# Another order of the seven Strassen products in a fused GAT and attention kernel

## The chip, the cores and the metric

The kernel runs on one core of one Trainium2 chip. The metric is device time in microseconds of one execution, the median of several runs. TensorE (PE) does matrix products, its weight loads are shown apart (PEld), VectorE (DVE), ScalarE (ACT) and GpSimd (POOL) do the elementwise work, and SyncE (SP) issues most of the transfers; ACT issues some as well.

## The reference

64 graphs of 256 nodes with 256 features pass through two layers, all in fp32.

```python
# layer 0, graph attention, adj is 0 or 1
h = gat(gat(x, adj, W1, a1), adj, W2, a2)          # softmax over nodes of leaky_relu scores, masked by adj
h = layernorm(x + h, g_ln1, b_ln1)
x = layernorm(h + relu(h @ w_ff1 + b_ff1) @ w_ff2 + b_ff2, g_ln2, b_ln2)     # 256 -> 1024 -> 256
# layer 1, attention of 8 heads with a value matrix per relation r
q, k = x @ Wq + bq, x @ Wk + bk
attn = softmax(q @ k.T / sqrt(32))
out = sum_r (attn * (adj == r)) @ (x @ Wv[r] + bv[r])
x = layernorm(x + out @ Wo + bo, g1, beta1)
out = layernorm(x + gelu(x @ W1 + b1) @ W2 + b2, g2, beta2)
```

With entries of 0 and 1 only two of the four relations occur, and the kernel has a path for that, `narrow_path`, which is the one that runs; a check of the data decides at its end whether the general path must follow.

## The kernel before, in words

A unit is two graphs, that is 512 rows in four blocks of 128. There are 32 units. `turn(y_, x_, z)` (L1226) works on three neighbouring units at once: the attention and the second feed-forward layer of unit y, the first feed-forward layer of unit x = y + 1, and the graph attention of unit z = y + 2. So each turn has three independent streams, whose pieces are interleaved by hand. The last two turns lack z, or z and x. A prologue (L1498 to L1532) brings the first units in.

The order is written out. `manual_schedule` (L1271) keeps the program's order on PE, SP, DVE and ACT within a turn that has a unit x; POOL is ordered by the planner, and around the border between two turns DVE and ACT of both may interleave. [...]A transfer issued by ACT stands in ACT's queue as well.

Three kinds of matrix product are done by Strassen's scheme, seven products of half-size quarters instead of eight: the projections q/k and v (`Projections`, L1006), the first half of each feed-forward layer (`hidden_seven`, L869) and its second half (`HiddenOut`, L957, not changed). Four sums of quarters are taken on the moving side beforehand (L880 to L886 and L1017), the sums of weights once at the start.

In `hidden_seven` the products come in halves a and b. Each half has two PSUM banks. Bank `two` receives product 2, then, overwritten, 5, and 3 is accumulated onto 5. Bank `one` receives 1, then 6, 7 and 4 accumulated onto it. The four output quarters (o, b) arise from what is read out between the products: quarter (0,0) is 2 (copied by ACT, L907) plus 1 (added by DVE, L910); quarter (1,1) is 5 (copied) plus bank one after 7 (added); quarter (0,1) is bank two after 3 (copied) plus bank one after 6 (added); quarter (1,0) is bank one after 4. A product may enter a bank only when the reader of what stood there is done. Then comes the function, ReLU in the first layer and Gelu in the second: "r" applies it to (0,0) and (0,1) of a half in two activations of 512 columns (L941), "s" to quarter (1,1) in two of 256 columns (L916), and product 4 is read through the function directly. The names "2a", "7b" in the order strings are product and half; each is two matrix multiplies (four PE records in the trace). For q and v, "q5" or "v6" name the same products of `Projections.step` (L1042); copies and adds have lines L1036 and L1040.

The places where the order is written: L1278 to L1309 for the projections together with quad 0 of the scores (`scores`, `powers` for the exponentials on ACT, L1093; `masks` for the multiplies by adjacency, L1097, and `totals`, L1102, on DVE), the calls of `first(...)` from L1322 to L1351 for unit x's first layer, and `second(...)` from L1438 to L1458 for unit y's second layer. Around these stand layer norms: `moments` and `norm` (L820, L830) with statistics on DVE and a power on POOL, `offsets` (L843) on DVE, `applied_norm` (L847) on ACT or, for two blocks of unit x, on POOL.

The transposed features hT that a layer multiplies are made by `normed_features` (L689): DVE transposes blocks of 32 by 32 (L694), then twelve transfers and four POOL copies put the pieces in place. For the first layer all twelve transfers are issued by SP, for the second layer (L1407) six by SP and six by ACT, after ACT has done `scaled` (L789) for unit z.

Of the kernel before, what the change touches and what calls it, by code (L numbers as in the profile page):

```python
# [16 lines left out]
P = 128  # L17
# [368 lines left out]
def narrow_path(  # L386
# [443 lines left out]
    def norm(u, l, y, blocks=range(T), mv=None):  # L830
# [3 lines left out]
        mv = moments(u, l, y, blocks if mv is None else blocks[len(blocks) // 2:], mv)  # L834
# [34 lines left out]
    def hidden_seven(u, l, hT, w, bi, func, d, tt):  # L869
# [39 lines left out]
        def added(h, o, b):  # L909
            mark["added"] = nc.vector.tensor_tensor(out(h, o, b), pair(one[h]), out(h, o, b), ALU.add)  # L910
# [8 lines left out]
        def step(name):  # L919
# [5 lines left out]
            elif n == "1":  # L925
                one[h] = bank(f"h1a{u}_{l}_{h}")
                product(one[h], h, a11, quarter[0][0], True)
                added(h, 0, 0)
# [4 lines left out]
            elif n == "3":  # L933
                product(two[h], h, s4, quarter[1][1], False)
                copied(h, 0, 1, two[h])
            elif n == "6":
                product(one[h], h, s2, moving(1), False)
                added(h, 0, 1)
# [3 lines left out]
            elif n == "7":  # L942
                product(one[h], h, s3, moving(2), False)
                added(h, 1, 1)
            elif n == "s":
                done(h, 1, 1)
            else:
                product(one[h], h, a22, moving(3), False)
                done(h, 1, 0, one[h])
# [56 lines left out]
    class Projections:  # L1006
# [31 lines left out]
        def added(s, x, o, b):  # L1038
            y = s.out(x, o, b)
            mark["projected"] = nc.vector.tensor_tensor(y, s.one[x].rearrange("p (i n) -> p i n", i=2), y, ALU.add)  # L1040

        def step(s, x, n):  # L1042
# [12 lines left out]
            if n == 2:  # L1055
                s.copied(x, 0, 0, ps)
                s.added(x, 0, 0)
            elif n == 5:
                s.copied(x, 1, 1, ps)
            elif n == 3:  # L1060
                s.copied(x, 0, 1, ps)
            elif n == 6:
                s.added(x, 0, 1)
            elif n == 7:
                s.added(x, 1, 1)
            elif n == 4:
                s.copied(x, 1, 0, ps)
# [158 lines left out]
    def turn(y_, x_, z):  # L1226
# [46 lines left out]
        with order:  # L1273
# [4 lines left out]
            p("q1 v1 q2")  # L1278
            if X:
                applied_norm(X["y"], *n, [0])  # L1280
            p("v2")
            if X:
                applied_norm(X["y"], *n, [1])
            p("q5")
            if X:
                applied_norm(X["y"], *n, [2])
                applied_norm(X["y"], *n, [3])
                X["hT"] = normed_features(x_, 0, X["y"])
            scores(0, (0,))
            p("v5")  # L1290
            powers(0, (1,))
            if z + 1 < NG:
                load_x(z + 1)
            p("q3 v3")
            powers(0, (2, 3))
            if waiting:
                w, wy = waiting[0]
                last = moments(w, 3, wy, range(NB))
            if X:
                masks(0, (0,))  # L1300
            p("q6 v6 q7 v7")
            if X:
                masks(0, (2,))
# [5 lines left out]
            p("q4 v4")  # L1309
            if waiting:  # L1310
                last = norm(w, 3, wy, mv=last)
            steps = first_hidden(x_) if X else None
            if waiting:
                offsets(*last)
            scores(1)
            masks(1)
# [12 lines left out]
            sums(1)  # L1329
            if X:  # L1330
                shares(0)
            first("3a 6a", 1)
# [4 lines left out]
            first("2b 1b")  # L1337
            masks(2, (2,))
            first("5b 7a 3b ra 6b")
            totals(2)  # L1340
            first("4a 7b rb")
# [4 lines left out]
            first("sa sb", 2)  # L1346
# [50 lines left out]
            if Z:  # L1397
# [3 lines left out]
                Z["m"].scaled(WH)  # L1401
            if X:
# [31 lines left out]
            if X:  # L1434
                out.add(4)
                n = norm(x_, 1, X["y"], mv=n)
            h1 = Y["h1"] = work.tile([P, FB, TN], F32, tag="h1", name=f"h1{y_}_1", bufs=1)
            second("2a 1a 2b 1b")  # L1438
            second("5a 5b")
            if X:  # L1440
                offsets(*n)
                applied_norm(X["y"], *n, [0])
            if Z:
                affine(y, rg3, rb3)
            second("3a")
            if X:
                applied_norm(X["y"], *n, [1])
            second("3b")
            if X:
                applied_norm(X["y"], *n, [2, 3], True)  # L1450
            second("6a 6b ra rb 7a 7b")
            if X and not Z:
                affine(y, rg3, rb3)
            if Z:
                X["hT"] = normed_features(x_, 1, X["y"], natural=True)
            elif X:
                X["hT"] = with_ones(to_features(X["y"], f"h2T{x_}", (nc.vector.tensor_copy,) * 2))
            second("sa sb 4a 4b")  # L1458
# [130 lines left out]
```

## Time and profile before

| | us |
|---|---|
| median of 3 runs | 3044.08 (3042.89 to 3045.79) |
| the profiled execution's own time | 3043.91 |
| its span, first to last instruction | 3042.3 |
| PE busy | 3000.0 |
| DVE busy | 2645.7 |
| ACT busy | 1684.9 |
| POOL busy | 679.8 |
| one copy of a bank, ACT, 128x512 (L907) | 0.585 |
| one add of a bank, DVE, 128x512 (L910) | 0.685 |
| one mask multiply, DVE, 128x1024 pairs (L1097) | 1.237 |
| one exponential, ACT, 128x512 (L1093) | 0.600 |

Busy means that the engine executed something; PE's weight loads overlap its multiplies and are shown apart. The ends of multiplies are modelled, so a busy PE may hold short waits. The chain is followed back from the last instruction to what released each step; it says which work set the end. A view of waits gives, for each engine and line, what ended the time before it. The mean granted clock of TensorE was 0.995.

### The profile page before, as it was taken

To read this page: it belongs to the slowest core of one execution; us is meant where nothing else is said; L and a number is where in the kernel's file an instruction comes from. 1 tells how busy PE (TensorE), PEld (TensorE's weight loads), DVE (VectorE), ACT (ScalarE), POOL (GpSimd) and SP (SyncE) were. 2 spreads that over 40 slices of the span, in tenths; PEclk is the share of its full clock that TensorE was granted. 3 is DMA by queue.
4 is the path that set the end of the run, shared out by engine and by line. 5 is a ranking of instruction groups with operands and counts; after the bars stand their busy time and mean duration, and the time that the engine had idled before them with its cause. 6 is when DMAs were issued, how large, how long until landed. Compare 5 with 4: busy or idle time off the path is not lost.

```text
span 3042.3 us, 58414 instructions
## 1 busy us (share of the span) xinstructions
PE 3000.0 (99%) x22192; PEld 2459.6 (81%) x22192; DVE 2645.7 (87%) x5025; ACT 1684.9 (55%) x3404; POOL 679.8 (22%) x930
## 2 busy tenths in 40 slices
PE   7999999999999999999999999999999999999998
PEld 6788888888787888787888878887878887878876
DVE  5788988888898889898889888898988898988887
ACT  4455555655655555555555455556555555555553
POOL 4222221222211222212222112222112222122211
PEclk8999999999999999999999999999999999999999
DMA  5011111211111211111111112111112111121000
GB/s 147 13 35 36 37 39 25 44 37 39 34 35 32 44 37 39 33 27 43 40 37 36 40 25 44 38 39 33 34 35 44 36 38 35 25 45 37 19 13 16
DMA packets 428402, 113.24 MB, mean 37 GB/s; under 512 B 364586, under 2 KB 427604, under 8 KB 428116
## 3 DMA queue, kind: packets, MB, share of 16 engines
q1 hardware_dynamic: 418076, 102.20, 15.3%
q10 hardware_dynamic: 8984, 6.19, 0.8%
q8 instruction: 178, 2.92, 0.4%
q0 software_dynamic: 1056, 1.05, 0.1%
q14 instruction: 108, 0.88, 0.1%
HBM read 56.78 MB, written 16.78 MB: 24 GB/s over the span
## 4 chain that ended last, share of the span: by engine, by line
PE 90%; DVE 7%; ACT 1%; DMA 1%; POOL 1%; issue 0%; SPq 0%; DVEq 0%; POOLq 0%; ACTq 0%
PE yf L987 22%; PE h1a L898 15%; PE h1b L898 12%; PE po L1112 8%; PE qk L1053 7%; PE v L1053 7%; PE sp L1084 4%; PE xpp L740 4%; PE yop L811 4%; PE ygp L811 3%; PE zo L1115 2%; PE hpp L800 2%; DVE s L775 2%; DVE yt L694 1%; DVE eaq L973 1%; DVE y L995 1%
## 5 line engine op out<-in xcount | busy, mean ns | idle before, releaser
L907 ACT COPY h<-h1b 128x512 f32<-128x512 f32 x384 | 224.5, 585 | 349.4 <-PE h1b L898 342.6
L910 DVE TENSOR_TENSOR h<-h1a,h 128x512 f32<-128x512 f32 x384 | 262.9, 685 | 114.6 <-PE h1a L898 108.8
L1097 DVE TENSOR_TENSOR ea<-e,aT 128x1024 f32<-128x1024 f32 x256 | 311.2, 1237 | 2.9 <-ACT e L1093 2.6
L855 ACT ACTIVATE y<-y,nm,rs 128x256 f32<-128x256 f32 x450 | 249.8, 597 | 114.4 <-DVE nm L845 110.1
L1093 ACT ACTIVATE e<-sp 128x512 f32<-128x512 f32 x512 | 270.8, 600 | 28.1 <-PE sp L1084 21.4
L1036 ACT COPY qk<-qk 128x512 f32<-128x512 f32 x128 | 75.1, 587 | 339.0 <-PE qk L1053 339.0
L711 POOL COPY hT<-yt 32x256 f32<-32x256 f32 x244 | 203.2, 833 | 184.9 <-DVE yt L694 172.6
L837 POOL TENSOR_SCALAR rs<-mv 128x4 f32<-128x4 f32 (+1 forms) x134 | 33.3, 248 | 841.0 <-DVE mv L827 625.3
L826 DVE BATCH_NORM_STATS2 st<-y 128x6 f32<-128x256 f32 x512 | 207.3, 407 | 4.5
L995 DVE TENSOR_TENSOR y<-yf,y 128x256 f32<-128x256 f32 x448 | 183.2, 409 | 29.5 <-PE yf L987 29.4
L1125 POOL TENSOR_TENSOR low<-low,rq 128x16 f32<-128x16 f32 x64 | 13.9, 218 | 810.4 <-DVE rq L1124 810.4
L867 DVE TENSOR_TENSOR y<-y,rb 128x1024 f32<-128x1024 f32 (+1 forms) x130 | 167.0, 1284 | 3.2
L941 ACT ACTIVATE h<-h,cols 128x512 f32<-128x512 f32 x256 | 167.0, 714 | 1.5 <-DVE h L910 1.1
L864 DVE TENSOR_TENSOR y<-y,rg 128x1024 f32<-128x1024 f32 (+1 forms) x130 | 161.6, 1243 | 1.2 <-ACT y L855 1.1
L1102 DVE TENSOR_TENSOR es<-e 128x1024 f32<-128x1024 f32 x128 | 155.8, 1217 | 0.0
L703 POOL COPY hT<-yt 32x256 f32<-32x256 f32 x120 | 114.9, 958 | 169.3 <-DVE yt L694 165.1
L838 POOL TENSOR_TENSOR rs<-rs,mhalf 128x4 f32<-128x4 f32 (+1 forms) x134 | 146.9, 1096 | 8.3
L1084 PE MATMUL sp<-qk 32*128 32x256 f32 x2048 | 146.6, 400 | 0.4 <-DVE qk L1040 0.3
L742 ACT COPY xp<-xpp 128x260 f32<-128x260 f32 x128 | 45.4, 385 | 172.6 <-PE xpp L740 172.5
L694 DVE STREAM_TRANSPOSE yt<-y 128x256 f32<-128x256 f32 x364 | 136.0, 418 | 4.5
L1112 PE MATMUL po<-e,v 128*32 128x256 f32 x2048 | 136.3, 384 | 0.0
L898 PE MATMUL h1a<-tt,wf 128*128 128x256 f32 x512 | 134.2, 386 | 0.3 <-DVE h L910 0.3
(280 smaller groups left out, 7589.6 us busy)
## 6 DMA issues: line engine op xcount, KB each, us to landing
hT<-yt SPq DMA_DIRECT2D x912, 32.0 KB, 1.9
y<-in_x_dram SPq DMA_DIRECT2D x32, 512.0 KB, 4.5
xq<-in_x_dram SPq DMA_DIRECT2D x240, 64.0 KB, 2.1
aq<-in_adj_dram SPq DMA_DIRECT2D x240, 64.0 KB, 2.3
out_dram<-y SPq DMA_DIRECT2D x30, 512.0 KB, 2.9
hT<-yt ACTq DMA_DIRECT2D x180, 32.0 KB, 1.9
wf<-in_L_gnn_w_ff_dram SPq DMA_DIRECT2D x2, 1024.0 KB, 7.6
w<-in_L_gnn_W_dram SPq DMA_DIRECT2D x2, 1024.0 KB, 7.9
```

The source lines that it names most:

```text
L811: nc.tensor.matmul(ps[:, i * F:(i + 1) * F], lhs(t, k), rhs(b, k), start=(k == 0), stop=(k == n - 1))
L855: mark["normed"] = nc.scalar.activation(y[:, t, :], y[:, t, :], AF.Identity, bias=nm[:, t:t + 1], scale=rs[:, t:t + 1])
L898: nc.tensor.matmul(ps[:, i * N:(i + 1) * N], w_[:, f * P:(f + 1) * P], m, start=first and i == 0, stop=True, skip_group_check=True)
L907: mark["copied"] = nc.scalar.copy(out(h, o, b), pair(ps))
L910: mark["added"] = nc.vector.tensor_tensor(out(h, o, b), pair(one[h]), out(h, o, b), ALU.add)
L987: nc.tensor.matmul(s.ps[n][:, i * F2:(i + 1) * F2], a[:, k, i * P:(i + 1) * P], w_[:, k, :], start=n in (1, 2, 5) and i == 0 and k == 0, s ...
L995: mark["out"] = nc.vector.tensor_tensor(yq, s.ps[n][:, :F].rearrange("p (i f) -> p i f", i=NB), yq, ALU.add)
L1053: nc.tensor.matmul(ps[:, i * N:(i + 1) * N], l, r, start=n in (1, 2, 5) and i == 0, stop=True, skip_group_check=True)
L1084: nc.tensor.matmul(ps[a][:, j * N:(j + 1) * N], k_[hp, m, j0:j0 + P], q[hp, m, b * N:(b + 1) * N], start=True, stop=True)
L1093: nc.scalar.activation(e[:, a, :], ps[a], AF.Exp, scale=isd)
L1097: nc.vector.tensor_tensor(ea[:, a:a + 2, :], e[:, a:a + 2, :], ab[:, None, :].to_broadcast([P, 2, NB * N]), ALU.mult)
L1112: nc.tensor.matmul(po[hp, m * N:(m + 1) * N], vs[:, hp], w[:, a, j * N:(j + 1) * N], start=(n == 0), stop=(n == len(terms) - 1))
```

## The change

The sixth product's bank is copied into quarter (0,1) and the third product's bank is added to it, where before the third was copied and the sixth added. So 6 can come before 3, and the order strings change: in both feed-forward layers and in the projections. In the second layer Gelu is applied per quarter: "c" to (0,0), "d" to (0,1) and "s" to (1,1), two activations of 256 columns each, and an activation of one column with Gelu is issued right after `scaled`. The norms, masks, moments and the transposes of features around these products move as well; `norm` gets an argument that says which blocks still lack statistics.

```diff
--- before.py
+++ after.py
@@ -827,11 +827,11 @@
             nc.vector.bn_aggr(mv[:, t, :], st[:, t, :])
         return mv
 
-    def norm(u, l, y, blocks=range(T), mv=None):
+    def norm(u, l, y, blocks=range(T), mv=None, rest=range(NB, T)):
 
         n, t0 = f"{u}_{l}_{blocks[0]}", blocks[0]
         bt = slice(t0, t0 + len(blocks))
-        mv = moments(u, l, y, blocks if mv is None else blocks[len(blocks) // 2:], mv)
+        mv = moments(u, l, y, blocks if mv is None else rest, mv)
         rs = work.tile([P, T], F32, tag="rs", name=f"rs{n}")
         nm = work.tile([P, T], F32, tag="nm", name=f"nm{n}")
         nc.gpsimd.tensor_scalar(rs[:, bt], mv[:, bt, 1], EPS, 0.0, op0=ALU.add, op1=ALU.add)
@@ -906,8 +906,8 @@
 
             mark["copied"] = nc.scalar.copy(out(h, o, b), pair(ps))
 
-        def added(h, o, b):
-            mark["added"] = nc.vector.tensor_tensor(out(h, o, b), pair(one[h]), out(h, o, b), ALU.add)
+        def added(h, o, b, ps):
+            mark["added"] = nc.vector.tensor_tensor(out(h, o, b), pair(ps), out(h, o, b), ALU.add)
 
         def done(h, o, b, ps=None):
             for i in range(2):
@@ -925,25 +925,25 @@
             elif n == "1":
                 one[h] = bank(f"h1a{u}_{l}_{h}")
                 product(one[h], h, a11, quarter[0][0], True)
-                added(h, 0, 0)
+                added(h, 0, 0, one[h])
             elif n == "5":
                 product(two[h], h, s1, moving(0), True)
                 copied(h, 1, 1, two[h])
                 mark["fifth"] = mark["copied"]
             elif n == "3":
                 product(two[h], h, s4, quarter[1][1], False)
-                copied(h, 0, 1, two[h])
+                added(h, 0, 1, two[h])
             elif n == "6":
                 product(one[h], h, s2, moving(1), False)
-                added(h, 0, 1)
+                copied(h, 0, 1, one[h])
             elif n == "r":
                 for f in range(2 * h, 2 * h + 2):
                     nc.scalar.activation(d["h1"][:, f, :], d["h1"][:, f, :], func, bias=bi[:, f:f + 1])
             elif n == "7":
                 product(one[h], h, s3, moving(2), False)
-                added(h, 1, 1)
-            elif n == "s":
-                done(h, 1, 1)
+                added(h, 1, 1, one[h])
+            elif n in "cds":
+                done(h, *{"c": (0, 0), "d": (0, 1), "s": (1, 1)}[n])
             else:
                 product(one[h], h, a22, moving(3), False)
                 done(h, 1, 0, one[h])
@@ -1035,9 +1035,9 @@
         def copied(s, x, o, b, ps):
             nc.scalar.copy(s.out(x, o, b), ps.rearrange("p (i n) -> p i n", i=2))
 
-        def added(s, x, o, b):
+        def added(s, x, o, b, ps):
             y = s.out(x, o, b)
-            mark["projected"] = nc.vector.tensor_tensor(y, s.one[x].rearrange("p (i n) -> p i n", i=2), y, ALU.add)
+            mark["projected"] = nc.vector.tensor_tensor(y, ps.rearrange("p (i n) -> p i n", i=2), y, ALU.add)
 
         def step(s, x, n):
             a11, a12, a22, s1, s2, s3, s4 = wqks if x == "q" else wvs
@@ -1052,19 +1052,8 @@
                 l, r = (w[:, i * P:(i + 1) * P], m) if x == "q" else (m[:, i * P:(i + 1) * P], w)
                 nc.tensor.matmul(ps[:, i * N:(i + 1) * N], l, r, start=n in (1, 2, 5) and i == 0, stop=True,
                                  skip_group_check=True)
-            if n == 2:
-                s.copied(x, 0, 0, ps)
-                s.added(x, 0, 0)
-            elif n == 5:
-                s.copied(x, 1, 1, ps)
-            elif n == 3:
-                s.copied(x, 0, 1, ps)
-            elif n == 6:
-                s.added(x, 0, 1)
-            elif n == 7:
-                s.added(x, 1, 1)
-            elif n == 4:
-                s.copied(x, 1, 0, ps)
+            to = {1: (0, 0), 2: (0, 0), 5: (1, 1), 6: (0, 1), 3: (0, 1), 7: (1, 1), 4: (1, 0)}[n]
+            (s.added if n in (1, 3, 7) else s.copied)(x, *to, ps)
 
         def __call__(s, names):
             for n in names.split():
@@ -1275,45 +1264,40 @@
             if X:
                 n = X.pop("n")
                 offsets(*n)
-            p("q1 v1 q2")
+            p("q2 v2 q1 v1")
             if X:
-                applied_norm(X["y"], *n, [0])
-            p("v2")
-            if X:
-                applied_norm(X["y"], *n, [1])
+                applied_norm(X["y"], *n, [0, 1, 2, 3])
+                X["hT"] = normed_features(x_, 0, X["y"])
             p("q5")
-            if X:
-                applied_norm(X["y"], *n, [2])
-                applied_norm(X["y"], *n, [3])
-                X["hT"] = normed_features(x_, 0, X["y"])
-            scores(0, (0,))
-            p("v5")
-            powers(0, (1,))
+            scores(0, (0, 1))
             if z + 1 < NG:
                 load_x(z + 1)
-            p("q3 v3")
-            powers(0, (2, 3))
             if waiting:
                 w, wy = waiting[0]
                 last = moments(w, 3, wy, range(NB))
+            p("v5 q6")
+            powers(0, (2,))
+            p("v6")
+            powers(0, (3,))
             if X:
-                masks(0, (0,))
-            p("q6 v6 q7 v7")
+                masks(0)
+            p("q3 q7")
+            p("v7")
             if X:
-                masks(0, (2,))
                 totals(0)
             else:
                 with behind("projected"):
                     masks(0)
                     totals(0)
-            p("q4 v4")
+            p("v3 q4 v4")
+            steps = first_hidden(x_) if X else None
             if waiting:
                 last = norm(w, 3, wy, mv=last)
-            steps = first_hidden(x_) if X else None
+            scores(1)
+            masks(1, (0,))
             if waiting:
                 offsets(*last)
-            scores(1)
-            masks(1)
+            masks(1, (2,))
             totals(1)
             if Z:
                 early(z)
@@ -1327,23 +1311,24 @@
                 first("2a 1a 5a", 1)
             scores(2)
             sums(1)
+            first("6a")
             if X:
                 shares(0)
-            first("3a 6a", 1)
+            first("3a", 1)
             if not X:
                 with behind("out"):
                     shares(0)
             masks(2, (0,))
-            first("2b 1b")
+            first("2b ra 1b 7a")
             masks(2, (2,))
-            first("5b 7a 3b ra 6b")
+            first("5b sa 6b 4a")
             totals(2)
-            first("4a 7b rb")
+            first("3b rb 7b")
             if X:
                 times(X["y"], rg1)
                 plus(X["y"], rb1)
             scores(3)
-            first("sa sb", 2)
+            first("sb", 2)
             masks(3)
             totals(3)
             if Z:
@@ -1399,6 +1384,7 @@
                 Z["m"].masks(1)
                 Z["m"].shares()
                 Z["m"].scaled(WH)
+                nc.scalar.activation(work.tile([P, 1], F32, tag="ve", name=f"ve{y_}"), mhalf[:, 0:1], AF.Gelu)
             if X:
                 out(6)
                 if not Z:
@@ -1433,29 +1419,28 @@
             second = hidden_seven(y_, 1, hT, w1s, b1, AF.Gelu, Y, tt.rearrange("p a n -> p (a n)"))
             if X:
                 out.add(4)
-                n = norm(x_, 1, X["y"], mv=n)
+                n = moments(x_, 1, X["y"], range(NB, NB + 1), n)
             h1 = Y["h1"] = work.tile([P, FB, TN], F32, tag="h1", name=f"h1{y_}_1", bufs=1)
-            second("2a 1a 2b 1b")
-            second("5a 5b")
+            second("2a 1a")
+            if X:
+                n = norm(x_, 1, X["y"], mv=n, rest=range(NB + 1, T))
+            second("2b 1b ca 6a")
             if X:
                 offsets(*n)
                 applied_norm(X["y"], *n, [0])
+                applied_norm(X["y"], *n, [2, 3], True)
+            second("5a")
+            if X:
+                applied_norm(X["y"], *n, [1])
             if Z:
                 affine(y, rg3, rb3)
-            second("3a")
-            if X:
-                applied_norm(X["y"], *n, [1])
-            second("3b")
-            if X:
-                applied_norm(X["y"], *n, [2, 3], True)
-            second("6a 6b ra rb 7a 7b")
+            second("6b 5b cb")
+            if Z:
+                X["hT"] = normed_features(x_, 1, X["y"], natural=True)
+            second("7a 7b sa sb 3a da 3b db 4a 4b")
             if X and not Z:
                 affine(y, rg3, rb3)
-            if Z:
-                X["hT"] = normed_features(x_, 1, X["y"], natural=True)
-            elif X:
                 X["hT"] = with_ones(to_features(X["y"], f"h2T{x_}", (nc.vector.tensor_copy,) * 2))
-            second("sa sb 4a 4b")
             if y_ >= NG - 2:
                 pieces = out_pieces(y_, y, h1)
                 if X:
@@ -1519,7 +1504,7 @@
         load_x(2)
         load_rows(2)
         load_adjacency(2)
-        first_hidden(0)("2a 1a 2b 1b 5a 5b 3a 3b 6a ra 6b rb 7a sa 7b sb 4a 4b")
+        first_hidden(0)("2a 1a 2b 1b 6a 5a 6b 5b 7a 7b sa sb 3a ra 3b rb 4a 4b")
         first = HiddenOut(0, 0, g[0]["y"], g[0]["h1"], wf2s, out_sums(0, 0))
         first.sums(1, 2, 4, 3)
         first(1, 2, 5, 6, 3)
```

## The prediction

> **What bounds the kernel now.** I read the page's busy shares and its chain first, then the chain in order of time through one turn (1033 to 1126 us; a turn is one pass of the unit loop, 92.4 us), then the waits, then the timelines of ScalarE (ACT), VectorE (DVE) and the queues. From the page, the busy shares and the chain by engine:
>
> ```profile
> PE 3000.0 (99%) x22192; PEld 2459.6 (81%) x22192; DVE 2645.7 (87%) x5025; ACT 1684.9 (55%) x3404; POOL 679.8 (22%) x930
> ...
> PE 90%; DVE 7%; ACT 1%; DMA 1%; POOL 1%; issue 0%; SPq 0%; DVEq 0%; POOLq 0%; ACTq 0%
> ```
>
> TensorE sets the end. Idle between its records is only 42 us, most of it in the first and last slices, so what can be gained lies inside "busy": pieces that last longer than their floor. In the chain in order of time (start, us, what), one Strassen product is "x4" and 0.86 us:
>
> ```profile
> 1035.23 0.86 PE qk L1053 x4
> 1036.10 0.86 PE v L1053 x4
> 1036.96 0.94 PE qk L1053 x4
> ...
> 1041.85 0.86 PE qk L1053 x4
> 1042.71 0.86 PE v L1053 x4
> 1043.57 1.12 PE qk L1053 x4
> 1044.70 0.86 PE v L1053 x4
> 1045.56 1.05 PE qk L1053 x4
> ...
> 1060.90 0.94 PE h1b L898 x4
> 1061.85 0.86 PE h1a L898 x4
> 1062.71 0.94 PE h1b L898 x4
> 1063.65 2.85 PE h1a L898 x12
> ```
>
> The extra tenths are waits for a bank to be read before the next product may go into it. The view of waits names them (total, times, longest):
>
> ```profile
> PEld h1a L898 <- DVE h L910: 37.4, 99, 0.7
> PEld h1b L898 <- ACT h L907: 26.8, 125, 0.3
> PEld qk L1053 <- DVE qk L1040: 22.8, 63, 0.7
> ```
>
> [...]product 7 of the queries starts at 1043.57, 0.06 after the add that reads its bank ends (1042.82 + 0.69). [...]The trace shows the load (1.28 us at 1104.81) but Gelu begins at 1106.10[...]. [...]I take 1.28 us[...].
>
> **The change, part by part.** Sums are per turn, for the 30 turns that carry a following unit.
>
> *Products, what goes.* Bank one now runs 1, 6, 7 or 1, 6, 7, 4 with one or more foreign products between each reader and the next writer, bank two 2, 5, 3 likewise.
> Projections: the excess of q5, v3, q7, q4 is 0.08 + 0.08 + 0.26 + 0.19 = 0.61 us. With the new order the nearest pair has two products (1.7 us) between, against 0.6 to 0.7 us for a copy or add plus some 0.2 of latency.
> First layer (ReLU): 5b 0.08, 3b 0.08, 7b 2.85 - 3 x 0.86 = 0.27, together 0.43; 5a keeps its 0.08.
> Second layer (Gelu): pieces of 3.53 and 5.63 us for four and six products, 0.09 + 0.47 = 0.56, less rounding 0.54.
> Removed: 0.61 + 0.43 + 0.54 = 1.58 us.
>
> *Projections, what comes.* Time from the first product (1033.34). The four norms now stand on ACT before q5's copy: the offsets end at 2.7 (as now), norms run 2.8 to 4.8 (0.5 apart), q5's copy to 5.3, two exponentials to 6.6 (scores start at 4.3, first exponential 1.17 later as at 1047.40/1048.57), v5's copy 7.15, q6's copy 8.1, third exponential 8.6, v6's copy 9.1, fourth 9.6. DVE has both mask multiplies of quad 0 ahead of q3's and q7's adds: the second needs the fourth exponential, so 9.6 to 10.8, q3's add to 11.4, q7's add to 12.0. TensorE wants q4 at 11.6 (7 products of q and v after q5's scores). So q4 waits about 0.4 us; v7's add (12.65) is in time for v4. Cost 0.4; bounds 0 (exponentials earlier) to 0.9. Projections net -0.2.
>
> *First layer, what comes.* 6a now is the first product after sums(1), and it needs 1a's add. In front of that add DVE has, in order: subtractions (wait for hT by DMA), two moments, a mask, the offsets, a mask, totals, the 1.24 us transpose. Transposes of hT end 0.7 us earlier than now (6.1 instead of 6.8), so the 12 SP transfers (7.54 us, landing 1.9 after issue) end about 15.0. Subtractions 15.05 to 16.6, moments 17.65 (they stood before the subtractions, in a hole; now behind), mask 18.8, offsets at 19.4 because POOL's add, high and power (0.24 + 0.32 + 1.02) follow the moments, mask 20.7, totals 21.8, transpose 23.0, 1a's add 23.6. TensorE arrives at 23.4: 0.2 us. In 4 of 30 turns now the subtractions wait 0.95 to 1.4 us for the transfer; there 6a would lose about 1.5, or 0.2 a turn on average. Cost 0.35; bounds 0 to 1. Net -0.08. From then on adds and copies meet their products with 0.15 us to spare or more (6b the tightest).
>
> *Second layer, what comes.* The one-column Gelu stands on ACT behind scaled(), so its table load does too, and behind both stand six of hT's twelve transfers (ACT queue), then four hp copies. Timeline of a usual turn (ACT's queue, then TensorE's first product of the layer):
>
> ```profile
> 1182.24 3.73 ACTq L713 DMA_DIRECT2D hT<-yt  x6
> ...
> 1189.27 1.03 PE L898 MATMUL h1b<-hT,w 128*128 128x256 f32 x4
> ```
>
> The last transfer starts at 1185.35 and lands at 1187.3, 2.0 us before TensorE needs it. The load delays the issue from 1182.24 to about 1184.06 (last scaling ends 1182.7, 1.28 load, small Gelu), by 1.8 us: landing 1189.1, just in time. In about 6 of 30 turns the subtractions here already wait over 1 us for the transfers, which leaves no such margin; there I expect 1.2 to 1.5, 0.3 a turn on average. The subtractions shift by 1 us, 1a's add ends 2.9 us after 2a's start, and 6a wants it at 3.46. The applied norms, affine (2.6 us) and the transposes stand before 7a's add on DVE; POOL's two norms (2.95 us) end 8.3 after 2a, transposes 9.1, 7a's add 9.8; 4a wants it at 10.4. Gelu per quarter: 8 activations of 256 columns (3.4 us from 1.69 for four) for 4 of 512 (2.56): 0.8 us more of ACT, hidden, since ACT now starts two of them early; quarter (0,1) is done at 12.9, the sum of quarters for product 5 at 14.15, wanted at 14.33. I charge 0.05 there. Without the early start those 0.8 us would fall on product 5. Cost 0.35, bounds 0 to 1.3. Net -0.19.
>
> *At nothing.* load_x is issued some places later, but its eight transfers stay behind hT's twelve on SP and wait for the early transpose there (8.2 us in SP's waits) in both orders; nothing on SP is late through it. hT for the next projections is transposed some 3 us earlier (9 instead of 12 us after 2a), and is wanted 29 us after 2a, so its 8.4 us of SP transfers stay hidden; without that cover each turn would pay for them.
>
> **Sum.** -1.58 + 0.4 + 0.35 + 0.35 = -0.48 us a turn, x 30 = -14, and -2 from the prologue's one layer and the last two turns, whose projections and layers have no late transfer and give some 0.5 us each: -16. The profiled execution is 3043.91 us (span 3042.3 and 1.6 around it), 0.2 below the median 3044.08. 3044 - 16 = 3028.
>
> **Rivals.**
> A (full gain): exponentials or DMA come early enough that none of the new waits is felt: 1.58 x 30 = 47, 2997 us. For it: each new wait is a few tenths. Against: three independent queues would all have to be early.
> B (no difference): DVE, busy 87%, takes the place of the bank waits: q4's wait 0.9 and 6a's 0.8 instead of 0.4 and 0.35 give -1.58 + 2.05 = +0.5 in the worst turns and around zero on average: 3038 to 3050. For it: DVE is back to back from the masks to 1a's add. Against: its free stretches before q5 and hT.
> C (slower): hT of the second layer. Place: the table load in front of ACT's six transfers.[...] It decides from a landing 0.78 us after TensorE's arrival, that is a delay of 2.7 us in a usual turn. For it: hp copies and transfers queue behind the load.[...]
> That the ring order does not shorten anything is excluded only if the waits in the view above are what stretches the pieces; the 0.06 us between add and product says so.
>
> **Numbers.** Likeliest (some new waits, net gain): 0.57, 3028, own range 3005 to 3037. A 0.09. B 0.10. C and other late transfers 0.24. Within 0.2% (6 us) is what a measurement of this kernel cannot tell from no change. Faster 0.66, same 0.10, slower 0.24. The range leaves out the far ends of A and C: 2999 to 3058.
>
> **What would show it.** Right: in the chain, q7, 3b, 5b, 7b and the second layer's h1a at 0.86 us a product; q4 near 1.3 with DVE's add as releaser; 6a up to 1.3 after zo; the second layer's subtractions starting about 1 us later than now and 2a still without idle; two table loads a turn, one behind scaled(). Wrong: if q4's or 6a's wait is over 1 us, or 2a waits for DMA in most turns, the gain is gone; if the table load appears somewhere other than before the transfers, the second layer gives its whole 0.54.

## The result, and the profile after

The changed kernel takes 3063.86 us (median of 4, 3056.92 to 3064.92) against 3043.94: a ratio of 1.006 (95% interval 1.0043 to 1.0077), slower by 20 us where 16 us faster was forecast. Its profiled execution is the quickest of the four, 3056.92 us (span 3055.3, 13.0 above the span before); a second profile follows below.

From the page of the changed kernel, the busy shares and the chain by engine:

```profile
PE 2966.2 (97%) x22192; PEld 2496.0 (82%) x22192; DVE 2614.3 (86%) x5025; ACT 1718.4 (56%) x3562; POOL 638.3 (21%) x930
...
PE 67%; DVE 17%; SPq 6%; DMA 3%; POOL 3%; issue 2%; ACT 1%; ACTq 0%; DVEq 0%; POOLq 0%
```

TensorE is busy 34 us less (3000.0 before): most of the bank waits that were counted as busy are gone. But its share of the chain falls from 90 to 67%: nearly a quarter of the chain has moved to work that TensorE waits for. In the chain in order of time (start, us, what), one turn shows which work:

```profile
1327.29 1.83 DMA hT<-yt
...
1330.76 0.35 DVE st L826
...
1332.03 1.00 POOL rs L837
1333.03 0.16 POOL high L840
1333.20 0.99 POOL rs L838
...
1334.29 1.22 DVE ea L1086
1335.51 1.14 DVE es L1091
1336.65 1.16 DVE xT L1128
1337.80 0.59 DVE h L910
...
1338.43 1.13 PE h1a L898 x4
```

From the last transfer of hT to product 6a (the last line) nothing but VectorE and GpSimd: subtractions (left out here), moments, GpSimd's three operations, mask multiply, totals, transpose, 1a's add. From the next product on each has its 0.86 us again. The view of waits names the two places where TensorE now waits for an add of VectorE, 6a and the fourth product of the queries, q4:

```profile
PE h1a L898 <- DVE h L910: 23.2, 31, 2.9
PEld qk L1053 <- DVE qk L1040: 21.6, 31, 0.7
```

To see where the time went I cut each turn at the starts of TensorE's groups and took the differences to the kernel before, summed over turns 1 to 29, with the stretch up to the end of turn 0, turn 30 (no unit z) and turn 31 (no z, no x) apart. Each row is one profiled execution; the rows of the experiments below are in the same table. "Projections" is the stretch from a turn's first product to the scores of head pair 1, "6a" the one from the scores of head pair 2 to the next product of the first layer, "hT" the one from the start of the first layer's second half to the second layer's first product.

| us against before | projections | 6a | rest of first layer | hT | second layer | other | to turn 0 | turn 30 | turn 31 | span |
|---|---|---|---|---|---|---|---|---|---|---|
| changed | -2.1 | +22.6 | -12.5 | +6.8 | -15.5 | +2.0 | +2.7 | +4.3 | +4.7 | +13.0 |
| changed, again | -2.1 | +22.9 | -12.5 | +12.4 | -13.7 | +1.9 | +5.6 | +4.4 | +4.9 | +23.8 |
| Gelu behind transfers | -2.1 | +22.6 | -12.5 | -0.1 | -16.0 | +0.5 | -0.4 | +6.2 | +4.7 | +2.9 |
| moments first | -2.1 | 0.0 | -12.5 | +9.7 | -15.3 | +1.9 | +3.2 | +5.1 | +6.2 | -3.8 |
| transpose first | -2.1 | +1.0 | -12.5 | +12.1 | -12.1 | +1.6 | +2.8 | +4.3 | +4.6 | -0.3 |
| offsets late | -2.1 | +12.0 | +3.5 | +7.6 | -15.6 | +1.9 | +3.3 | +5.9 | +4.7 | +21.1 |
| second mask late | -18.4 | +39.6 | -12.5 | +5.4 | -15.4 | +1.6 | +2.6 | +3.8 | +5.8 | +12.6 |
| ends | -2.1 | +22.7 | -12.5 | +6.9 | -13.9 | +1.2 | +1.2 | +5.0 | +2.6 | +11.1 |
| first layer only | 0.0 | +2.3 | -12.5 | 0.0 | 0.0 | -0.1 | -1.2 | -0.4 | +0.3 | -11.6 |
| second layer only | -0.9 | 0.0 | -0.3 | +10.0 | -13.9 | +2.5 | +1.2 | +2.8 | +4.2 | +5.6 |
| three groups | -2.1 | 0.0 | -12.5 | +0.7 | -15.7 | -0.1 | -1.8 | +2.1 | +1.6 | -27.8 |
| three groups and q4 | -18.4 | +0.2 | -12.5 | +0.1 | -15.9 | -0.3 | -2.2 | -0.1 | +1.8 | -47.4 |
| that, no early Gelu | -18.4 | +0.1 | -12.5 | -0.2 | -4.4 | -1.1 | -1.3 | +1.5 | +1.8 | -34.5 |

The two layers give what was forecast (-12.5 and -15.5). 6a takes +22.6, the projections give almost nothing, and the ends (the three columns before the span) cost 11.7 where -2 was booked.

### The profile page after: what moved, and what is told of

Read it like the earlier page. It is cut to its first block, busy times and chain, and to the rows that moved or that the text cites. A ratio compares the mean times of both kernels' runs of the same rounds, so it can differ in the third digit from the quotient of the medians.

```text
span 3055.3 us, 58545 instructions
## 1 busy us (share of the span) xinstructions
PE 2966.2 (97%) x22192; PEld 2496.0 (82%) x22192; DVE 2614.3 (86%) x5025; ACT 1718.4 (56%) x3562; POOL 638.3 (21%) x930
## 3 DMA queue, kind: packets, MB, share of 16 engines
q1 hardware_dynamic: 418076, 102.20, 15.3%
q8 instruction: 178, 2.92, 0.4%
## 4 chain that ended last, share of the span: by engine, by line
PE 67%; DVE 17%; SPq 6%; DMA 3%; POOL 3%; issue 2%; ACT 1%; ACTq 0%; DVEq 0%; POOLq 0%
PE yf L987 21%; PE h1a L898 13%; PE h1b L898 9%; SPq L713 6%; PE po L1101 4%; PE xpp L740 4%; PE yop L811 4%; PE ygp L811 3%; DVE yt L694 3%; PE qk L1053 2%; DMA hT<-yt 2%; PE v L1053 2%; DVE s L775 2%; DVE tt L881 2%; PE sp L1073 1%
## 5 line engine op out<-in xcount | busy, mean ns | idle before, releaser
L855 ACT ACTIVATE y<-y,nm,rs 128x256 f32<-128x256 f32 x450 | 242.6, 593 | 163.0 <-DVE nm L845 158.3
L907 ACT COPY h<-h1b 128x512 f32<-128x512 f32 x256 | 149.0, 582 | 214.2 <-PE h1b L898 206.3
L837 POOL TENSOR_SCALAR rs<-mv 128x4 f32<-128x4 f32 (+1 forms) x134 | 56.3, 420 | 963.7 <-DVE mv L827 833.7
L916 ACT ACTIVATE h<-h,cols 128x256 f32<-128x256 f32 x512 | 222.3, 502 | 36.7 <-DVE h L910 36.7
L711 POOL COPY hT<-yt 32x256 f32<-32x256 f32 x244 | 207.4, 850 | 151.2 <-DVE yt L694 140.1
L910 DVE TENSOR_TENSOR h<-h1a,h 128x512 f32<-128x512 f32 x256 | 170.0, 677 | 35.5 <-PE h1a L898 31.6
L1114 POOL TENSOR_TENSOR low<-low,rq 128x16 f32<-128x16 f32 x64 | 13.9, 217 | 755.4 <-DVE rq L1113 755.4
L1101 PE MATMUL po<-ea,v 128*32 128x256 f32 x2048 | 135.9, 379 | 0.0
L987 PEld LDWEIGHTS yf<-wf,eaq 128*128 128x128 f32 x1024 | 119.1, 192 | 16.3 <-DVE eaq L973 15.0
L740 PE MATMUL xpp<-gwe,xT 128*128 128x260 f32 x512 | 128.7, 396 | 3.8 <-ACT xT L675 3.8
```

The costliest lines, as they stand in the source:

```text
L711: nc.gpsimd.tensor_copy(to, at)
L740: nc.tensor.matmul(ps[:, :WX], hT[k][:, t * P:(t + 1) * P], gwe[:, k, :], start=(k == 0), stop=(k == KB - 1))
L855: mark["normed"] = nc.scalar.activation(y[:, t, :], y[:, t, :], AF.Identity, bias=nm[:, t:t + 1], scale=rs[:, t:t + 1])
L916: nc.scalar.activation(y, y if ps is None else ps[:, i * N:(i + 1) * N], func, bias=bi[:, f:f + 1])
L987: nc.tensor.matmul(s.ps[n][:, i * F2:(i + 1) * F2], a[:, k, i * P:(i + 1) * P], w_[:, k, :], start=n in (1, 2, 5) and i == 0 and k == 0, s ...
L1101: nc.tensor.matmul(po[hp, m * N:(m + 1) * N], vs[:, hp], w[:, a, j * N:(j + 1) * N], start=(n == 0), stop=(n == len(terms) - 1))
```

## Experiments

### The changed kernel again

> The changed kernel once more, unchanged, for its level and for a second profile. If the profiled execution of 3057 is typical in its middle, the turns again take 92.5 us and the ends (the stretch before the first projections, the turn behind the last masked one, the last turn) are again some 13 us longer than before. Rival: the time is set in the middle. Executions at 3064 then have more turns in which the second layer's first product waits for the transfers of hT: over 0.5 us a turn on average, instead of 0.25.

Measured: 3064.89 us (3061.19 to 3067.70); the profiled execution took 3067.70. Both parts of the expectation hold something: the ends are again longer (5.6 + 4.4 + 4.9), and hT costs 12.4 instead of 6.8. The turns are very uneven: in most, the second layer starts on time, in nine of turns 0 to 29 it is 0.5 to 2.6 us late. hT and the ends make 8.8 of the 10.8 us between the spans of the two profiles, and the second layer, which gives 1.8 less, most of the rest.

### The one-column Gelu behind the transfers

```diff
                 Z["m"].scaled(WH)
-                nc.scalar.activation(work.tile([P, 1], F32, tag="ve", name=f"ve{y_}"), mhalf[:, 0:1], AF.Gelu)
...
                     hT = normed_features(y_, 2, y, queues=(nc.sync, nc.scalar))
+                    nc.scalar.activation(work.tile([P, 1], F32, tag="ve", name=f"ve{y_}"), mhalf[:, 0:1], AF.Gelu)
```

> The changed kernel with the one-column Gelu behind the six transfers that ScalarE issues, instead of before them. Theory (the table load makes hT late): the stretch from the end of the feed-forward output to the second layer goes back from 17.0 to 16.8 us in every turn, and the kernel becomes 7 us faster than the changed one (0.25 x 30), more where an execution had many late turns: 3050 to 3057. Rival (the late turns are the transfers' own scatter): late turns stay as many and the time stays within 3 us of the changed kernel's.

Measured: 3048.15 us (3046.15 to 3051.48), 16.7 less than the changed kernel, measured in the same series (3064.89), and 2 below the expected range. The hT column goes to -0.1, and no turn's second layer is more than 0.1 us late: the load's place is what makes hT late, though not in every turn, as the expectation had it. Against the second profile of the changed kernel the gain lies in hT (12.5) and in the stretch to turn 0 (6.0), where hT had been 2.0 us late.

But the load alone doesn't make it late. The timeline of the changed kernel (ScalarE, its queue, the transfers) in a turn on time:

```profile
1370.68 0.54 ACTq L713 DMA_DIRECT2D hT<-yt  x1
...
1371.15 1.28 ACT L1387 ACT_TABLE_LOAD   x1
1371.26 0.60 ACTq L713 DMA_DIRECT2D hT<-yt  x1
1372.44 0.20 ACT L1387 ACTIVATE ve<-mhalf 128x1 f32<-128x1 f32 x1
1372.76 2.49 ACTq L713 DMA_DIRECT2D hT<-yt  x4
```

and in one that is 1.3 us late:

```profile
1924.97 0.52 ACTq L713 DMA_DIRECT2D hT<-yt  x1
...
1925.44 1.28 ACT L1387 ACT_TABLE_LOAD   x1
1925.53 0.60 ACTq L713 DMA_DIRECT2D hT<-yt  x1
...
1928.59 2.87 ACTq L713 DMA_DIRECT2D hT<-yt  x4
...
1933.31 0.89 PE L898 MATMUL h1b<-hT,w 128*128 128x256 f32 x3 [1.15 <-DMA hT<-yt]
```

Two of the six transfers go out before the load is done; the other four begin 0.9 us after those in the first case, 2.5 us in the second. The view of DMA of the late turn (1924.2 to 1931.2) has a queue that the turn on time (1370 to 1377) hasn't:

```profile
q8 instruction: 1, 0.02, 0.8%
```

The view gives "instruction" as the kind of this queue; one of its packets is called an instruction packet here. Take the stretch from 9.5 to 15 us after TensorE's `rows` products (L749) that precede the second layer, in turns 0 to 29. In the changed kernel 13 turns have such a packet there (in this queue or in q14, the other of that kind), and nine of them are over 0.1 us late; of the 17 without one, none is. In all eight profiles with the Gelu ahead of the transfers, 65 turns are late, all 65 with a packet. In the kernel before and in this experiment there are as many packets (15 and 13 turns), and no turn is more than 0.22 us late.

The issue times narrow it down. In 56 of the 57 late turns other than turn 0, one of ScalarE's last four transfers is issued 0.5 to 2.1 us later than in the usual turn of its profile, 0.3 to 1.4 us after a packet has ended; in 40 of the 57 SyncE's issue slips by over 0.3 us too. In the kernel before, ScalarE's issue slips beside packets as well: by up to 0.96 us in turns on time, by 1.50 in the one late turn. So two things meet: the load puts off four transfers by 0.84 us (4.57 for the six instead of 3.73), which takes most of their slack (about 1 us by the slips in the kernel before), and an issue that then slips beside an instruction packet makes hT late. That the packet causes the slip was not shown: the times agree with it, but no run took the packets away. In turn 0, which is 2.0 to 2.1 us late in all eight, the issue slips 0.6 us before the packet begins, so there something else starts it.

In the whole execution the page of the changed kernel lists two queues of this kind: q8 with 178 packets and 2.92 MB (16.4 KB each), q14 with 111 and 0.90 MB (8.1 KB each).

### Moments ahead of the subtractions

```diff
-            steps = first_hidden(x_) if X else None
             if waiting:
                 last = norm(w, 3, wy, mv=last)
+            steps = first_hidden(x_) if X else None
```

> The changed kernel with the moments and the norm of the last layer of the unit before (and so GpSimd's three operations) ahead of the subtractions of the first layer on VectorE, where they stood before the change. Theory: the wait of product 6a goes, the stretch from the scores of head pair 2 to the next product of the layer falls from 4.17 to about 3.4 us, -0.75 x 30 = -22 us: 3035 to 3042. Rival (VectorE is simply full there, the order of its work doesn't matter): 6a waits as long as now and the time is within 5 us of the changed kernel's. A second rival: the moments ahead delay the subtractions where hT is early, and the first layer's start pays 0.3 us or more.

Measured: 3040.21 us (3032.90 to 3043.01), 24.7 less than the changed kernel and within the expected range. The 6a column goes from +22.6 to 0.0; the start of the layer doesn't move. VectorE isn't too full; the order of its work decides.

### Transpose ahead of the mask multiplies

```diff
+            if Z:
+                early(z)
             scores(1)
             masks(1, (0,))
...
             totals(1)
-            if Z:
-                early(z)
```

> The changed kernel with VectorE's 1.24 us transpose of the next inputs (one operand in SBUF) between the moments and the first mask multiply of head pair 1, instead of behind the totals. Theory[...]: GpSimd's first operation runs beside the transpose, in 0.23 us instead of 1.00, the offsets wait 0 to 0.3 us instead of 1.27, 1a's add comes 0.6 to 1 us earlier and 6a's wait falls from 0.80 to 0.2 or less: -15 to -20 us, 3045 to 3050. Rival (the operation is slow beside any work of VectorE): 1.00 us as before, and the time within 4 us of the changed kernel's.

The timelines of VectorE and GpSimd, first of the changed kernel:

```profile
1331.75 1.19 DVE L1086 TENSOR_TENSOR ea<-e,aT 128x1024 f32<-128x1024 f32 x1
...
1332.03 1.00 POOL L837 TENSOR_SCALAR rs<-mv 128x4 f32<-128x4 f32 x1 [8.97 <-DVE mv L827]
...
1334.21 0.16 DVE L845 SCALAR_TENSOR_TENSOR nm<-mv,rs 128x4 f32<-128x4 f32 x1 [1.27 <-POOL rs L838]
```

then with the transpose first:

```profile
1325.30 1.21 DVE L1128 STREAM_TRANSPOSE xT<-xq 128x1024 f32<-128x1024 f32 x1
...
1325.58 0.23 POOL L837 TENSOR_SCALAR rs<-mv 128x4 f32<-128x4 f32 x1 [8.96 <-DVE mv L827]
1325.78 0.19 POOL L840 TENSOR_TENSOR high<-high,mv 128x4 f32<-128x4 f32 x1
1325.93 1.02 POOL L838 TENSOR_TENSOR rs<-rs,mhalf 128x4 f32<-128x4 f32 x1
```

Measured: 3042.97 us (3038.54 to 3045.29), 21 to 22 less than the changed kernel, slightly more than expected. GpSimd's first operation, with a one-operand operation of VectorE beside it, takes 0.23 us instead of 1.00, VectorE has no 1.27 us of idle time, and 6a's wait is gone (+1.0 over 29 turns). The rival, slow beside any work of VectorE, falls by the 0.23. The time alone would not decide. By an estimate from this timeline, with 1.00 for the first and the other two as long as here, GpSimd's three operations would have ended some 0.2 us after the mask multiply, since VectorE now has the transpose to do meanwhile, so most of the 1.27 us would have gone as well.

### Offsets behind the mask multiply and the totals

```diff
             masks(1, (0,))
-            if waiting:
-                offsets(*last)
             masks(1, (2,))
             totals(1)
+            if waiting:
+                offsets(*last)
```

> The changed kernel with VectorE's small operation that needs GpSimd's reciprocal root (the offsets) behind the second mask multiply and the totals of head pair 1 instead of ahead of them; the moments stay behind the subtractions. Theory (6a is late because VectorE stands 1.27 us idle for GpSimd, whose first operation takes 1.00 us instead of 0.23 beside the mask multiply): the idle time goes, 1a's add comes 1.2 us earlier, 6a's wait of 0.80 goes: 3040 to 3046. Rival (the moments' own 1.05 us in front are the cause, or the norms on ScalarE, now 1.2 us later, hold up the copies of the layer): less than 8 us gained.

Measured: 3069.52 us (3065.17 to 3074.12), a miss: 3040 to 3046 was expected, and it is not even faster than the changed kernel (3064.89). GpSimd's timeline says why:

```profile
1334.46 1.00 POOL L837 TENSOR_SCALAR rs<-mv 128x4 f32<-128x4 f32 x1 [8.96 <-DVE mv L827]
1335.44 1.13 POOL L840 TENSOR_TENSOR high<-high,mv 128x4 f32<-128x4 f32 x1
1336.52 2.01 POOL L838 TENSOR_TENSOR rs<-rs,mhalf 128x4 f32<-128x4 f32 x1
```

With three two-operand operations of VectorE back to back, now all three of GpSimd's take longer (1.00, 1.13 and 2.01 us, against 0.23, 0.19 and 1.02 in the experiment before): each begins beside one of them (0.91, 1.07 and 1.12 us left). VectorE still idles 0.92 us for the root and 6a gains only 0.37 us a turn. The rest of the layer takes 0.55 us more, as the rival had it: the norms on ScalarE come 1.9 us later, and a copy behind them, which VectorE's next add needs. I had taken GpSimd's time as given and moved the waiting; the cause was what ran beside it.

### The second mask multiply of head pair 0 behind the adds

```diff
             if X:
-                masks(0)
+                masks(0, (0,))
             p("q3 q7")
             p("v7")
             if X:
+                masks(0, (2,))
                 totals(0)
```

> The changed kernel with that last edit alone. Theory (the waits stand one behind the other on VectorE): q4's 0.45 us goes, but product 6a, which waits for VectorE's add of 1a, is ready no earlier, so its wait grows from 0.80 to about 1.2 us: within 5 us of the changed kernel's 3064.9. Rival (each wait has its price by itself): -13 us, 3052.

Measured: 3062.41 us (3056.58 to 3064.49), no difference: the projections give 16.3 us more and 6a takes 17.0 more. The chain above explains it: 6a's time is set from hT's transfers on, so time won on TensorE ahead of it is waited for there.

### The ends

`with_ones` takes the engine as an argument: VectorE before the first projections and in turn 30.

```diff
-        nc.gpsimd.memset(hT[KB - 1][one], 1.0)
+        engine.memset(hT[KB - 1][one], 1.0)
...
-            second("2b 1b ca 6a")
+            second("2b 1b ca 6a" if Z else "2b 1b 5a 5b ca 6a")
...
-            second("6b 5b cb")
+            second("6b 5b cb" if Z else "6b cb")
...
-            second("7a 7b sa sb 3a da 3b db 4a 4b")
+            second("7a 7b sa sb 3a da 3b db")
             if X and not Z:
                 affine(y, rg3, rb3)
-                X["hT"] = with_ones(to_features(X["y"], f"h2T{x_}", (nc.vector.tensor_copy,) * 2))
+                X["hT"] = with_ones(to_features(X["y"], f"h2T{x_}", (nc.vector.tensor_copy,) * 2), nc.vector)
+            second("4a 4b")
```

> The changed kernel with three edits at its ends only: the row of ones of the first hT and of that of the turn without a following masked unit written by VectorE instead of GpSimd; in that turn the transposes of hT ahead of the fourth products of the layer, as before the change; and in the two turns without a residual unit the fifth products ahead of the early activations and the sixth, as before. Theory (the ends lost 13 us): the first projections start at 104 us instead of 108, the last two turns lose 2 to 4 us each, together 9 to 12 us less than the changed kernel, with every turn between as now: 3045 to 3055. Rival (the ends only shift, what is gained there is waited for a few us later): less than 4 us.

Measured: 3054.89 us (3053.90 to 3056.32), 10 less. Not all of it is the ends: their three columns sum to 8.8 here, against 11.7 and 14.9 in the two profiles of the changed kernel, so the edits are worth 3 to 6 us, and the rest is the uneven hT (6.9, against 6.8 and 12.4). The first projections start at 105.9 us instead of 108.3 (expected 104), turn 31 gains 2.1, turn 30 nothing. There the changed kernel waits twice (TensorE's timeline, turn 30):

```profile
2952.17 1.13 PE L898 MATMUL h1a<-tt,w1s 128*128 128x256 f32 x4 [2.06 <-DVE h L910]
...
2965.38 1.91 PE L1053 MATMUL qk<-h2T,wqk 128*128 128x256 f32 x4 [3.42 <-POOL h2T L686]
```

and with the edits still waits for hT, behind VectorE's affine:

```profile
2965.60 1.62 PE L1053 MATMUL qk<-h2T,wqk 128*128 128x256 f32 x3 [3.85 <-DVE h2T L686]
```

So for turn 30 the rival was right: the first wait moved into the second. In the next kernels hT's copies stand ahead of the affine.

### One layer's order alone, on the kernel before

First layer (turns only): `hidden_seven` with the third product added and the sixth copied, and the order strings of the change.

> The kernel before with the new order of products in the first feed-forward layer of the 31 turns alone (the projections, the second layer and the layer of the prologue as before; the moments ahead of the subtractions as before). Theory (the layer's part is worth its bank waits): the stretch from 6a to the scores of head pair 3 falls from 9.26 to 8.83 us, with no wait for 6a, -0.43 x 31 = -13 us: 3028 to 3033. Rival (6a's early place costs by itself): more than 3036.

Measured: 3034.18 us (3032.28 to 3034.76), ratio 0.9966 (0.9954 to 0.9979). The 0.43 us a turn come, 6a costs 0.08 of them, and the time is 1 us above the expected range: alone and with the moments in their old place, this part of the change is a gain.

Second layer, with Gelu per quarter and the one-column Gelu as in the change.

> The kernel before with the new order of products in the second feed-forward layer alone, Gelu per quarter and the one-column Gelu ahead of the transfers included. Theory (the layer gives 0.53 us a turn and the table load takes 0.25 to 0.45 back, and the ends of the kernel 4 to 6 us): 3037 to 3046, no difference that counts. Rival (the table load is late only where the other parts have shifted the transfers): 3030 or less.

Measured: 3051.02 us (3049.11 to 3053.31), ratio 1.0023 (1.0013 to 1.0033): slower, outside the expected range. The layer gives 13.9, hT takes 10.0, as allowed (0.25 to 0.45 a turn), but the ends take 8.2 where 4 to 6 was allowed, and other stretches 2.5. The load's lateness doesn't need the other parts of the change.

### Together

The three groups of edits are those above; for the ends, the order with the fifth products first is in turn 31 alone, and in turn 30 hT's copies stand ahead of the affine and the fourth products.

> The changed kernel with three groups of edits at once: the one-column Gelu behind the six transfers, the moments and the norm ahead of the subtractions, and the ends (ones written by VectorE at the start and in the turn without a following masked unit; in that turn the copies of hT ahead of the fourth products' work and of the affine; in the last turn alone the fifth products ahead of the early activations). Theory (three causes apart from each other): the single gains of 16.7 and 24.7 us and 10 to 14 us for the ends add up, 3064.9 - 53 = 3008 to 3015, which is also what the removed bank waits of the two layers leave of the kernel before (3044 - 30 x 0.95 = 3016). Rival (the causes hide each other, a product that comes earlier waits at the next place): over 3022.

Measured: 3016.57 us (3015.31 to 3017.55), ratio 0.9909. The single gains of 16.7, 24.7 and 10 sum to 51; 48 came, 1.6 us short of the expected range. So the causes hardly hide each other, though the single gains overlap in part: the 10 of the ends holds some of the uneven hT.

> The kernel of the three groups of edits, and also the second mask multiply of head pair 0 behind the adds of q3, q7 and v7 on VectorE instead of ahead of them. Theory (q4 waits for VectorE, which waits for the fourth exponential): the gap from v3 to q4 falls from 1.32 to 0.87 us, -0.45 x 30 = -13 us against the kernel of the three groups: 2995 to 3002. Rival (the mask, the totals and v3's add, now later, are waited for at the next scores or at 6a): within 4 us of it.

Measured: 2996.51 us (2995.88 to 2997.23), ratio 0.9844 (0.983 to 0.9857), 20 less than the three groups, of which the projections' column gives 16.3 and turn 30 2.2: on a kernel without a wait at 6a, the same edit that gave nothing above gives its whole price. This version beats both kernels. In its chain in order of time the projections are nearly TensorE alone:

```profile
1297.33 0.86 PE v L1053 x4
1298.19 1.73 PE qk L1053 x8
1299.92 1.73 PE v L1053 x8
1301.64 0.86 PE qk L1053 x4
```

and by engine the chain of its page is back to that of before:

```profile
PE 90%; DVE 8%; DMA 1%; ACT 1%; POOL 0%; issue 0%; SPq 0%; DVEq 0%; POOLq 0%; ACTq 0%
```

> The best kernel so far (2996.5) without the one-column Gelu, so that the table is loaded at the first real Gelu of the second layer. Theory (the early load covers 1.28 us of ScalarE, which has some slack in that layer): the activations of the first quarter end 1.3 us later, the copies behind them too, and product 5 or 7 waits 0.3 to 0.8 us a turn: 3005 to 3020. Rival (ScalarE's slack covers it): within 4 us.

Measured: 3009.22 us (3006.58 to 3009.45), 12.7 more: the second layer takes 0.40 us a turn longer. So the early load is worth 12.7 us where it stands behind the transfers; ahead of them it cost 16.7 against that place, in the changed kernel, which is more than it is worth.

## Why the prediction was wrong, point by point

**Removed, 1.58 us a turn: right.** In the version without new waits the projections are 0.63 us a turn shorter (14.09 to 13.46), the first layer 0.43, the second 0.55, together 1.61 against 0.61 + 0.43 + 0.54. With the ends mended as well, the whole kernel then takes 2996.5; the full gain had been worked out as 2997.

**q4's wait, 0.4: right cause, too small.** From v3 to q4 it takes 0.46 us more than a product, and 0.56 went when the mask was moved. The projections were to give 0.2 and gave 0.07. Two lines of the timeline, the mask multiply waiting for the fourth exponential and q4 for VectorE's add:

```profile
1324.06 1.23 DVE L1086 TENSOR_TENSOR ea<-e,aT 128x1024 f32<-128x1024 f32 x1 [1.70 <-ACT e L1082]
...
1326.54 1.13 PE L1053 MATMUL qk<-tq,wqk 128*128 128x256 f32 x4 [0.30 <-DVE qk L1040]
```

**6a, 0.35: this step failed.** The list of what stands ahead of 1a's add was complete; one price was wrong, "POOL's add, high and power (0.24 + 0.32 + 1.02)". The add took 1.00 us in 30 of 30 turns, because the new order puts a mask multiply beside it. 6a's wait was 0.78 us on the average (22.6 over 29 turns): 0.36 in the turns with the earliest hT, up to 1.84 in the others, and longer by just as much as the subtractions began later. With the 0.77 us (1.00 - 0.23) taken off each turn, an estimated 0.17 would be left, less than was booked. The price came from the kernel before, where VectorE stood idle when this operation began, in all 29 turns. In the turn of the prediction (GpSimd, then VectorE):

```profile
1049.83 0.23 POOL L837 TENSOR_SCALAR rs<-mv 128x4 f32<-128x4 f32 x1 [6.98 <-ACT e L1093]
...
1050.95 0.42 DVE L881 TENSOR_TENSOR tt<-hT 128x256 f32<-128x256 f32 x1 [1.32 <-DMA hT<-yt]
```

In the changed kernel the add began in all 30 turns beside a mask multiply, whose two operands are in SBUF, with 0.91 to 0.92 us of it left, and took 0.09 us more than that. Beside adds with one operand in PSUM it took 0.23 to 0.24 (L910, up to 0.64 us left). The kernel before even showed it: this line's longest of 134 was 1050 ns against a median of 234, beside a sum of VectorE (L973) with 0.95 us left, and the 0.32 of the price was itself measured beside a subtraction (L881: 0.32 to 0.47 in 22 turns; 0.19 to 0.20 in the 11 with VectorE idle). What the operation waits for was not shown beyond these times.

**hT of the second layer, 0.35: right size, in part by luck.** The place was right, and so was the guess that a part of the turns would pay, those in which the transfers come late. But the issue is not 1.8 us late but 0.8, since two transfers pass the load (in all 30 turns), and what makes those turns late, issue that slips beside an instruction packet, was not in the prediction. A usual turn has no loss; the average is 0.23 a turn in the one profile, 0.43 in the other. The rival that ended slower named this place, but needed a delay of 2.7 us in a usual turn; the measured one was 0.84.

**Ends, -2: this step failed.** They cost 11.7 us in the first profile and 14.9 in the second. I had looked for late transfers only. At the start the first two products now need the half of hT with the row of ones, which GpSimd wrote behind 4.47 us of scaling; in turn 0 hT was 2.1 us late, which goes when the load stands behind the transfers; in turns 30 and 31 6a waited 2.06 and 2.85 us for VectorE, and turn 30 transposed its hT after the last product and then waited 3.42.

**The sum.** Against the forecast of -16: 6a 0.43 x 29 = +12, the projections 0.13 x 29 = +4, the ends +14; hT, the rest of the two layers and small stretches nearly cancel (-1, rounding included). That makes +13, the difference of the two spans. The seven further us of the median are hT's and the start's, as the second profile shows.

What stays open: how an instruction packet and the slip of the issue hang together, what makes turn 0 late, and why "other" is 2 us longer in the kernels with late hT.

## What to carry to other kernels

When an order is changed, price each moved small operation by what will run beside it, not by its median (1.00 us against 0.23 here): look at the longest of its row and ask when that happens. A gain ahead of a wait that another engine's chain set was worth nothing here until that chain was shortened; the same edit gave 0 and then 16 us. The load put ahead of the transfers in ScalarE's queue took 0.84 us of their slack, though the usual turn showed no loss.

## What was unexpected in the hardware

GpSimd's add on 4 columns (L837) took 0.23 to 0.25 us with VectorE idle (changed kernel) and 0.23 beside the transpose, which has one operand in SBUF. Begun beside a two-operand SBUF operation of VectorE, it took the rest of that one and 0.09 us (1.00), and GpSimd's next operation (`high`), with the offsets late, the rest and 0.06 (1.13 instead of 0.19). A power, 1.02 us with VectorE idle, took the rest and 0.89 there (2.01). In all 30 turns of the changed kernel two of the six transfers on ScalarE's queue were issued before the table load had ended, one 0.46 to 0.47 us before it began and one 0.09 to 0.18 after, although the Gelu that the load serves stands ahead of them in the program. An instruction packet (8.1 or 16.4 KB on the average) near the transfers goes with 0.1 to 2.9 us of delay in the eight profiles with the Gelu ahead of them: all 65 late turns have one, in turn 0 only after the slip had begun.
